# Moving the query's transposes and block sums into the second product, two scores forward, and one matrix load behind its scatters

## The chip, the cores and the metric

The kernel runs on one NeuronCore of a Trainium2 chip. It uses five engines with instruction streams of their own: TensorE (PE, matmuls and transposes), VectorE (DVE), ScalarE (ACT), GpSimd (POOL, here mostly gathers and scatters) and SyncE (SP, which issues most transfers). The metric is the device time of one execution in microseconds (us). Before the change it is 3199.84 us, the median of three runs (3196.97 to 3201.5).

## The reference, cut to what matters

Four graph layers, each with a residual and a layer norm, on x of 128 batches x 128 nodes x 256 features, all float32. Cut to the first layer, which the change touches, and its frame:

```python
# --- layer 0: attention over 512 edges, 4 heads of 64
Xq = (H @ W_lin.T).reshape(bt, n, h, dh)
Xv = (H @ W_val.T).reshape(bt, n, h, dh)
e = einsum('behd,hd->beh', leaky_relu(Xq[:, src] + Xq[:, dst], 0.2), a) + log(A0[src, dst] + EPS)
attn = exp(e - segment_max(e, src)) / segment_sum(...)       # softmax over the edges of one source
Y = segment_sum(attn * Xv[:, dst], src) ;  out = Y @ W_out.T
x = layernorm(x + out)
# --- layer 1: three products, each mixed over the nodes with adj * adj, relu after two of them
h = relu(mix(x @ W1)); h = relu(mix(h @ W2)); x = layernorm(x + mix(h @ W3))   # 256-512-1024-256
# --- layer 2: x @ W[k] for k = 0..2, mixed with diagonal, upper and lower triangle, + bias, layernorm
# --- layer 3: normalized adjacency, two linear maps with batch norm over all 128*128 rows, layernorm
```

## The kernel before

The 128 batches are worked in 32 quads of 4. A main loop has one round for each quad, and in round k five quads are in work at once: k-1 (`a`: layer 2, layer 3), k (`c`: second and third product of layer 1), k+1 (`b`: aggregation, first product), k+2 (`e`: scores and softmax) and k+3 (`g`: query and value product). The order of each engine's instructions is the order of the Python calls; waits between engines follow from the data.

Large products are done as seven block products in place of eight (Strassen-Winograd), with sums of blocks (S1 to S4, T1 to T4) made beforehand:

```python
class Seven:                      # y, z, x are PSUM banks; part() keeps a copy, out() writes a result
    def p1(self): self.y = ps("y"); self.mm(self.y, "A11", "B11", True); self.k1 = self.part(self.y, 0)
    def p5(self): self.z = ps("z"); self.mm(self.z, "S1", "T1", True)
    def p2(self): x = ps("x");      self.mm(x, "A12", "B21", True);      self.out(0, 0, x, self.k1)
    def p6(self): self.mm(self.y, "S2", "T2", False); self.k2 = self.part(self.y, 1)
    ...                           # p7, p4, p3 likewise

def values_in(k, xg, copy=None):  # transposes of x: 8 on PE into two banks, two copies on DVE
    for j in range(0, QB, 2):
        pt = ps("pt")...
        ... nc.tensor.transpose(pt[:, t, c, :], xg[:, j + t, c * P:(c + 1) * P], ident)      # L245
        xt = temp("xt")...;  copy(xt, pt);  s.xts.append(xt)                                 # L247

def node_blocks(tiles, room):     # the four sums of the left side, on DVE (L181 to L184)
    ...
    sums_a(a, a)

def queries(k, room):             # query and value product of quad k
    ...
    a = node_blocks(s.xts, room)
    def part(bank, i):
        nc.scalar.copy(room[2 + i], bank);  return room[2 + i]                               # L306
    return Seven(node_product(a, queries.blocks), part, out)

def temp(name):                   # six buffers
    return wk.tile([P, 512], F32, tag="t", name=name, bufs=6)
```

A score of one chunk of 128 edges is three DVE instructions on 128x1024 (the last chunk has one more):

```python
def score(k, c, weight=None):
    nc.vector.scalar_tensor_tensor(z, z, SLOPE, z, op0=ALU.mult, op1=ALU.max)                # L365
    nc.vector.tensor_mul(z3, z3, a_bc...)                                                    # L367
    nc.vector.reduce_sum(s.es[:, c, :], z..., axis=AX.X)                                     # L368
    ... elif c == NE - 1: nc.vector.tensor_add(s.es, s.es, log_col...)                       # L372
```

The attention weights are scattered into a matrix in DRAM and read back:

```python
def scatter(k, load=True):
    for c in range(NE): nc.gpsimd.indirect_dma_start(out=ad, ..., in_=s.at[:, c, :])         # L415
    if load: load_weights(k)      # nc.sync.dma_start(s.ad, ad...), 1 MB                     # L424
```

The second product of layer 1 has 14 block products, two halves g = 0, 1 of seven. Each is 4 matmuls of 512 columns (8 records of 256 columns in the profile). `between[i]` holds other work that is called at place i:

```python
def second(k, between):
    def keep(to, g, name):  to[g] = temp(name)...;  nc.scalar.copy(to[g], y[g])              # L578
    def total(g, row, col, bank, kept_): nc.vector.tensor_add(block(g, row, col), bank[g], kept_[g])  # L584
    def relu(g, row, col, src_=None): nc.scalar.activation(h, ..., AF.Relu)                  # L588

    product(y, 0, "A11", B11); keep(p1, 0, "p1");                                   after(0)
    product(y, 1, "A11", B11); keep(p1, 1, "p1");                                   after(1)
    product(x, 0, "A12", B21); total(0, 0, 0, x, p1);                               after(2)
    product(z, 0, "S1", T1);                                                        after(3)
    product(y, 0, "S2", T2);   keep(u2, 0, "u2");                                   after(4)
    product(y, 1, "S2", T2);   keep(u2, 1, "u2"); relu(0, 0, 0);                    after(5)
    product(x, 1, "A12", B21); total(1, 0, 0, x, p1);                               after(6)
    product(y, 0, "S3", T3);   keep(u3, 0, "u3"); total(0, 1, 1, z, u3); relu(1, 0, 0); after(7)
    product(z, 1, "S1", T1);                                                        after(8)
    product(y, 1, "S3", T3);   keep(u3, 1, "u3"); total(1, 1, 1, z, u3); relu(0, 1, 1); after(9)
    product(y, 0, "A22", T4);  relu(0, 1, 0, y[0]);                                 after(10)
    product(z, 0, "S4", B22);  total(0, 0, 1, z, u2); relu(1, 1, 1);                after(11)
    product(y, 1, "A22", T4);  relu(1, 1, 0, y[1]); relu(0, 0, 1);                  after(12)
    product(z, 1, "S4", B22);  total(1, 0, 1, z, u2); relu(1, 0, 1);                after(13)
```

One round, cut:

```python
def iteration(k):
    steps = softmax_parts(e)      # generator: [PE transpose L382, 4 ACT copies] [DVE scan L386] [scan L388]
                                  #   [DVE sub L391] [ACT exp L393] [DVE scan] [DVE scan]
    for i in (0, 1, 2, 3, 5, 7):          between[i] += [next(parts)]          # rest of layer 2 of quad a
    between[11] += [next(steps)];         between[12] += [next(steps)] * 2
    for c_, i in enumerate((0, 3, 6)):    between[i] += [score(e, c_ + 1)]
    for j, i in enumerate((5, 8, 9, 10)): between[i] += [by_row(b, j)]         # ACT copies, L434
    between[13] += [values_in(g, quads[g].xg)]
    second(c, between)
    quads[g + 1].xg = load_x(g + 1, "xg", 1, xpool)
    room = room_of("m2", 7)       # the buffer of the second product's right side, free from here on
    next(steps)
    q = queries(g, room[:5])
    stage_f(a)                    # PE L790 into two banks, two ACT copies (L793)
    h = hidden(a, room[5:] + room[2:4])   # layer 3, another seven block products (L819), its sums L188 to L191
    q.p1(); next(steps); run(q.p5, q.p2, q.p6); run(h.p1, h.p5); next(steps); q.p7(); ...
    spill(g)                      # query rows to DRAM (L268), then gather(g): 6 of the 8 gathers (L333)
    ...                           # aggregation, third product, first product, head of layer 2
```

Rounds 1 to 28 have a quad g, rounds 1 to 29 a quad e. The start, before the loop, does the first three quads by hand. Cut to what the change touches:

```python
    attention(0)
    scatter(0, False)
    ...                           # values(2, 0..3); the last one spills quad 2 (L268)
    values_in(3, quads[3].xg, nc.scalar.copy)
    quads[4].xg = load_x(4, "xg", 1, xpool)          # L205
    load_weights(0)                                  # L424
    score(1, 1, ...); ...
    for j in range(QB): by_row(0, j, ...)            # L434, on ACT and DVE by turns
    aggregate(0)                                     # PE L448
```

Of the kernel before, what the change touches and what calls it, by code (L numbers as in the profile page):

```python
# [26 lines left out]
def gnn_stack(ctx: ExitStack, tc: tile.TileContext, x, adj, w_qv_t, a, w_out_t, src, dst,  # L27
# [14 lines left out]
    nc = tc.nc  # L42
    B, N, D = x.shape
# [21 lines left out]
    def ps(name):  # L65
        return psum.tile([P, 512], F32, tag="ps", name=name)
# [62 lines left out]
    with ExitStack() as phase:  # L129
# [103 lines left out]
        def temp(name):  # L233
            return wk.tile([P, 512], F32, tag="t", name=name, bufs=6)
# [43 lines left out]
        def node_blocks(tiles, room):  # L278

            a = {f"A{j + 1}{c + 1}": tiles[j][:, :, c, :] for j in range(2) for c in range(2)}  # L280
            for i in range(4):
                a[f"S{i + 1}"] = room[i // 2][:, (i % 2) * 256:(i % 2 + 1) * 256].rearrange("p (b n) -> p b n", b=2)
            sums_a(a, a)
            return a

        def node_product(a, b):
            def mm(bank, i, j, new):
                for t in range(2):
                    nc.tensor.matmul(bank[:, t * 256:(t + 1) * 256], a[i][:, t, :], b[j],
                                     start=new and t == 0, stop=t == 1, skip_group_check=True)  # L290
            return mm
# [5 lines left out]

        def queries(k, room):

            s = quads[k]  # L300
            s.qt = wk.tile([P, QB, D], F32, tag="xb", name=f"qt{k}", bufs=1)
            s.xv = ws.tile([P, QB, D], F32, tag="xv", name=f"xv{k}", bufs=3)
            a = node_blocks(s.xts, room)

            def part(bank, i):
                nc.scalar.copy(room[2 + i], bank)  # L306
                return room[2 + i]

            def out(row, col, bank, kept_):
                to = (s.qt, s.xv)[col][:, 2 * row:2 * row + 2, :].rearrange("p b d -> p (b d)")  # L310
                if kept_ is None:
                    nc.scalar.copy(to, bank)
                else:
                    nc.vector.tensor_add(to, bank, kept_)

            return Seven(node_product(a, queries.blocks), part, out)

# [238 lines left out]
        def second(k, between):  # L556
# [3 lines left out]
            y, z, x = [None] * 2, [None] * 2, [None] * 2  # L560
            p1, u2, u3 = [None] * 2, [None] * 2, [None] * 2

# [12 lines left out]

            def keep(to, g, name):
                to[g] = temp(name).rearrange("p (i b n) -> p i b n", i=2, b=2)
                nc.scalar.copy(to[g], y[g])  # L578
# [15 lines left out]

            product(y, 0, "A11", B11)
            keep(p1, 0, "p1")
            after(0)
            product(y, 1, "A11", B11)
            keep(p1, 1, "p1")
            after(1)  # L600
# [5 lines left out]
            product(y, 0, "S2", T2)  # L606
            keep(u2, 0, "u2")
            after(4)
            product(y, 1, "S2", T2)
            keep(u2, 1, "u2")  # L610
            relu(0, 0, 0)
# [4 lines left out]
            product(y, 0, "S3", T3)  # L616
            keep(u3, 0, "u3")
            total(0, 1, 1, z, u3)
# [4 lines left out]
            product(y, 1, "S3", T3)  # L623
            keep(u3, 1, "u3")
            total(1, 1, 1, z, u3)
# [52 lines left out]
        def layer2(k, b):  # L678
# [52 lines left out]
            def mix(p):  # L731
                po = ps("po2").rearrange("p (t d) -> p t d", d=D)
                for i in range(2):
                    nc.tensor.matmul(po, split_t[:, i, :], g[p][:, :, (i + 1) * D:(i + 2) * D],
                                     start=(i == 0), stop=(i == 1))
                return po
# [22 lines left out]
            if b is not None:  # L759
                mixed(b, 2, pm[2])  # L760
                mixed(b, 3, pm[3])
            run(u.p1, u.p2, u.p5, u.p6, v.p1, v.p2, u.p7, v.p5, v.p6, u.p4, u.p3, v.p7)
            yield
            scaled(0)
# [114 lines left out]
        def run(*parts):  # L879
            for p in parts:  # L880
                p()

        def iteration(k):
# [11 lines left out]
            if has_c:  # L895
                between = {i: [] for i in range(14)}
                for i in (0, 1, 2, 3, 5, 7):
                    between[i].append(lambda: next(parts, None))
                between[11].append(lambda: next(steps, None))
                between[12] += [lambda: next(steps, None)] * 2  # L900
                if has_e:
                    for c_, i in enumerate((0, 3, 6)):
                        between[i].append(lambda c_=c_: score(e, c_ + 1))
                if has_b:
                    for j, i in enumerate((5, 8, 9, 10)):
                        between[i].append(lambda j=j: by_row(b, j))
                if has_g:
                    between[13].append(lambda: values_in(g, quads[g].xg))
                second(c, between)
# [8 lines left out]
            if has_g:  # L918
                q = queries(g, room[:5])
            stage_f(a)  # L920
# [123 lines left out]
        def start():  # L1044
# [136 lines left out]
            attention(0)  # L1181
            scatter(0, False)

# [28 lines left out]
            quads[4].xg = load_x(4, "xg", 1, xpool)  # L1212
            load_weights(0)
            score(1, 1, ends[:, 3, :])
# [343 lines left out]
```

## Time and profile before

| what | value |
|---|---|
| time, median of 3 | 3199.84 us |
| span of the profiled execution | 3199.8 us |
| TensorE clock granted, mean | 0.992 |
| one round, score transpose to score transpose | 87.37 us |
| ScalarE, GpSimd busy | 44%, 20% |
| memory traffic over the span | 105 GB/s |

The page of the profile shows the busy time of each engine and, for each kind of instruction, what ended the idle time before it. A line such as

```profile
L571 PE MATMUL ph<-m,w_s 128*128 128x256 f32 x1536 | 360.5, 381 | 11.9 <-DVE h L584 11.9
L578 ACT COPY u<-ph 128x512 f32<-128x512 f32 x128 | 74.9, 585 | 371.8 <-PE ph L571 371.8
L434 ACT COPY adc<-ad 128x512 f32<-128x512 f32 x126 | 134.9, 1071 | 8.3 <-DMA ad<-attd 8.3
```

reads: source line, engine and operation; output and inputs by name; shapes and number; then total busy time and the mean of one in ns; then the engine's idle time just before such instructions, and what ended it. The first is a part of the second product: 1536 matmuls of 381 ns as recorded (their records overlap, so the time from one start to the next is shorter), with 11.9 us of idle TensorE that ended when VectorE finished line 584. The second shows the other kind of waiting: ScalarE is idle 371.8 us before its copies, because it is ahead of TensorE. In the timeline, rows of the same kind are merged: start, duration, engine, line, names, shapes, number, and in brackets the idle time before and its end.

### The profile page before, as it was taken

How to read it: one execution, taken by the hardware profiler on the slowest of the kernel's cores; microseconds unless marked ns; L12 is line 12 of the kernel's file. 1: busy time of each engine (PE TensorE's matmuls, PEld its weight loads, DVE VectorE, ACT ScalarE, POOL GpSimd, SP SyncE). 2: the span in 40 equal slices, each digit the busy share in tenths (PEclk: the TensorE clock that was granted, in tenths of full speed). 3: DMA queues.
4: the chain of work that ended last, by engine and by line, in shares of the span. 5: the costliest groups of instructions: out<-in, count | busy, mean ns of one | idle time of the engine just before them, and what ended most of it. 6: DMA issues, size and time to landing. Idle time of an engine off the chain costs nothing. (4 is left out here: it accounts for less than half of the span.)

```text
span 3199.8 us, 39789 instructions
## 1 busy us (share of the span) xinstructions
PE 3105.5 (97%) x14760; PEld 2407.4 (75%) x14760; DVE 2301.8 (72%) x4598; ACT 1392.7 (44%) x2549; POOL 646.2 (20%) x533
## 2 busy tenths in 40 slices
PE   7999999999999999999999999999999999989998
PEld 3778887888888888888888888887888887864444
DVE  6777777777777777777777777777767776448888
ACT  3344433444444444433444444444433344326668
POOL 3211222222111111222222121111222220001135
PEclk8999999999999999999999999999999999999999
DMA  7423333333333323333333323323333331005557
GB/s 232 102 72 81 100 100 99 106 106 106 99 80 106 96 83 86 100 99 100 106 106 106 100 80 106 95 80 85 105 100 100 106 106 41 20 27 185 177 190 277
DMA packets 117472, 340.04 MB, mean 106 GB/s; under 512 B 14880, under 2 KB 51616, under 8 KB 108960
## 3 DMA queue, kind: packets, MB, share of 16 engines
q0 software_dynamic: 44400, 147.35, 18.9%
q1 hardware_dynamic: 71120, 189.23, 16.6%
q8 instruction: 117, 1.92, 0.2%
q10 hardware_dynamic: 1760, 0.92, 0.1%
q14 instruction: 75, 0.61, 0.1%
HBM read 252.00 MB, written 85.46 MB: 105 GB/s over the span
## 5 line engine op out<-in xcount | busy, mean ns | idle before, releaser
L571 PE MATMUL ph<-m,w 128*128 128x256 f32 x2048 | 473.1, 379 | 0.0
L652 PE MATMUL p<-w,h 128*128 128x256 f32 x2048 | 464.1, 380 | 0.0
L571 PEld LDWEIGHTS ph<-m,w 128*128 128x128 f32 x2048 | 386.8, 190 | 80.0 <-issue 14.8
L652 PEld LDWEIGHTS p<-w,h 128*128 128x128 f32 x2048 | 389.8, 190 | 67.1 <-issue 8.1
L333 POOL DMA_INDIRECT zs<-qd,src_idx x120 | 115.6, 963 | 1409.0 <-DMA qd<-qt 1275.5
L571 PE MATMUL ph<-m,w_s 128*128 128x256 f32 x1536 | 360.5, 381 | 11.9 <-DVE h L584 11.9
L571 PEld LDWEIGHTS ph<-m,w_s 128*128 128x128 f32 x1536 | 289.4, 190 | 75.0 <-DVE h L584 23.5
L333 POOL DMA_INDIRECT zs<-qd,dst_idx x120 | 189.4, 1578 | 346.9 <-DMA zs<-qd,src_idx 338.3
L578 ACT COPY u<-ph 128x512 f32<-128x512 f32 x128 | 74.9, 585 | 371.8 <-PE ph L571 371.8
L415 POOL DMA_INDIRECT attd<-at,att_idx x128 | 140.8, 1100 | 349.4 <-DMA attd<-at,att_idx 253.6
L113 ACT ACTIVATE ln_sd<-ln_mv,eps 128x2 f32<-128x2 f32 x192 | 56.0, 292 | 279.4 <-DVE ln_mv L108 279.4
L588 ACT ACTIVATE h<-h 128x512 f32<-128x512 f32 x192 | 121.0, 630 | 118.1 <-DVE h L584 118.1
L367 DVE TENSOR_TENSOR zs<-zs,a_bc 128x1024 f32<-128x1024 f32 x125 | 153.2, 1225 | 4.3
L368 DVE TENSOR_REDUCE scores<-zs 128x16 f32<-128x1024 f32 x125 | 152.5, 1220 | 4.3
L715 ACT COPY x2k<-y 128x384 f32<-128x384 f32 x192 | 91.8, 478 | 141.1 <-PE y L708 113.5
L365 DVE SCALAR_TENSOR_TENSOR zs<-zs 128x1024 f32<-128x1024 f32 x125 | 151.5, 1212 | 0.2 <-DMA zs<-qd,dst_idx 0.2
L106 DVE BATCH_NORM_STATS2 ln_st<-xr 128x6 f32<-128x256 f32 x384 | 144.6, 419 | 6.6
L121 DVE TENSOR_SCALAR xr<-xr,ln_mv,ln_rs 128x256 f32<-128x256 f32 x384 | 143.5, 416 | 7.0
L434 ACT COPY adc<-ad 128x512 f32<-128x512 f32 x126 | 134.9, 1071 | 8.3 <-DMA ad<-attd 8.3
L119 DVE RECIPROCAL ln_rs<-ln_sd 128x2 f32<-128x2 f32 x192 | 31.3, 163 | 148.0 <-ACT ln_sd L113 148.0
L676 POOL TENSOR_TENSOR xb<-xr,bias 128x512 f32<-128x512 f32 x64 | 99.1, 1548 | 168.3 <-DVE xr L121 150.8
L529 PE MATMUL pm<-wt_t,h 128*128 128x128 f32 x1024 | 128.8, 279 | 0.0
(336 smaller groups left out, 6144.7 us busy)
## 6 DMA issues: line engine op xcount, KB each, us to landing
ad<-attd SPq DMA_DIRECT2D x32, 1024.0 KB, 4.8
zd<-z SPq DMA_DIRECT2D x31, 1024.0 KB, 7.4
zl<-zd SPq DMA_DIRECT2D x62, 512.0 KB, 3.6
xr<-in_x_dram SPq DMA_DIRECT2D x32, 512.0 KB, 7.1
x3d<-xr SPq DMA_DIRECT2D x32, 512.0 KB, 2.6
x3l<-x3d SPq DMA_DIRECT2D x32, 512.0 KB, 5.1
out_dram<-x3l POOLq DMA_DIRECT2D x31, 512.0 KB, 5.7
qd<-qt SPq DMA_DIRECT2D x30, 512.0 KB, 2.6
```

Source lines behind the costliest of these rows:

```text
L106: nc.vector.bn_stats(st[:, i, :], r[:, i, :])
L121: nc.vector.tensor_scalar(r[:, i, :], r[:, i, :], mv[:, i, 0:1], rs[:, i:i + 1], op0=ALU.subtract, op1=ALU.mult)
L333: nc.gpsimd.indirect_dma_start(out=s.z[c], out_offset=None, in_=s.qd, in_offset=bass.IndirectOffsetOnAxis(ap=idx[:, c:c + 1], axis=0), com ...
L365: nc.vector.scalar_tensor_tensor(z, z, SLOPE, z, op0=ALU.mult, op1=ALU.max)
L367: nc.vector.tensor_mul(z3, z3, a_bc.unsqueeze(1).to_broadcast([P, QB, D]))
L368: nc.vector.reduce_sum(s.es[:, c, :], z.rearrange("p (r d) -> p r d", d=DH), axis=AX.X)
L415: nc.gpsimd.indirect_dma_start(out=ad, out_offset=bass.IndirectOffsetOnAxis(ap=att_idx[:, c:c + 1], axis=0), in_=s.at[:, c, :], in_offset= ...
L434: (copy or nc.scalar.copy)(s.adc[:, j * H:(j + 1) * H, :], s.ad.rearrange("p (s r) -> p r s", r=R)[:, j * H:(j + 1) * H, :])
L529: nc.tensor.matmul(pm[:, c // 2, c % 2, :], quads[k].h1[i, c], wt_t, start=True, stop=True)
L571: nc.tensor.matmul(bank[g][:, i].rearrange("p b n -> p (b n)"), wa[:, c, f:f + P], s.m2[:, blk_b, c].rearrange("p b n -> p (b n)"), start= ...
L588: nc.scalar.activation(h, h if src_ is None else src_, AF.Relu)
L652: nc.tensor.matmul(p3[:, t * D:(t + 1) * D], s.h2[f // 2][:, f % 2, j + t, :], w3_sb[:, f, :], start=(f == 0), stop=(f == K2 - 1))
```

## The change

It has four parts. The transposes of x for the next query product, and the four block sums made of them, move from behind the second product to its place 11, two block products before its end. The sums get two temporary tiles in place of the room that comes free only after the second product. The second and third of the three scores in the second product move from places 3 and 6 to places 2 and 4. In the start, the load of the first attention matrix goes directly behind its scatters in the queue, ahead of a spill and a load of x. To make the buffers come out, the kept tiles of the second product are taken all at once at its beginning, and the two PSUM banks for the mixing of layer 2 before it. No computation is added or removed. The aim is that TensorE finds its inputs ready.

```diff
-        def queries(k, room):
+        def queries(k, kept_at):
             s = quads[k]
+            blocks = quads[k].x_blocks
             ...
-            a = node_blocks(s.xts, room)
             def part(bank, i):
-                nc.scalar.copy(room[2 + i], bank)
-                return room[2 + i]
+                nc.scalar.copy(kept_at[i], bank)
+                return kept_at[i]
             ...
-            return Seven(node_product(a, queries.blocks), part, out)
+            return Seven(node_product(blocks, queries.blocks), part, out)
+
+        def query_sums(k):
+            quads[k].x_blocks = node_blocks(quads[k].xts, [temp("xs") for _ in range(2)])
 ...  # second()
-            p1, u2, u3 = [None] * 2, [None] * 2, [None] * 2
+            p1, u3, u2 = ([temp(name).rearrange("p (i b n) -> p i b n", i=2, b=2) for _ in range(2)]
+                          for name in ("p1", "u3", "u2"))
-            def keep(to, g, name):
-                to[g] = temp(name).rearrange("p (i b n) -> p i b n", i=2, b=2)
+            def keep(to, g):
                 nc.scalar.copy(to[g], y[g])
 ...  # layer2()
-                po = ps("po2").rearrange("p (t d) -> p t d", d=D)
+                po = pos[p]
 ...
             run(u.p1, u.p2, u.p5, u.p6, v.p1, v.p2, u.p7, v.p5, v.p6, u.p4, u.p3, v.p7)
+            pos = [ps("po2").rearrange("p (t d) -> p t d", d=D) for _ in range(2)]
             yield
 ...  # iteration()
                 between[11].append(lambda: next(steps, None))
+                if has_g:
+                    between[11] += [lambda: values_in(g, quads[g].xg), lambda: query_sums(g)]
 ...
-                    for c_, i in enumerate((0, 3, 6)):
+                    for c_, i in enumerate((0, 2, 4)):
                         between[i].append(lambda c_=c_: score(e, c_ + 1))
 ...
-                if has_g:
-                    between[13].append(lambda: values_in(g, quads[g].xg))
                 second(c, between)
 ...
-                q = queries(g, room[:5])
+                q = queries(g, room[:3])
 ...  # start()
-            scatter(0, False)
+            scatter(0)
 ...
             quads[4].xg = load_x(4, "xg", 1, xpool)
-            load_weights(0)
             score(1, 1, ends[:, 3, :])
```

More of the change, by code (lines that the diff above doesn't have):

```diff
@@ L595, in second @@
             product(y, 0, "A11", B11)
-            keep(p1, 0, "p1")
+            keep(p1, 0)
             after(0)
             product(y, 1, "A11", B11)
-            keep(p1, 1, "p1")
+            keep(p1, 1)
             after(1)
@@ L606, in second @@
             product(y, 0, "S2", T2)
-            keep(u2, 0, "u2")
+            keep(u2, 0)
             after(4)
             product(y, 1, "S2", T2)
-            keep(u2, 1, "u2")
+            keep(u2, 1)
             relu(0, 0, 0)
@@ L616, in second @@
             product(y, 0, "S3", T3)
-            keep(u3, 0, "u3")
+            keep(u3, 0)
             total(0, 1, 1, z, u3)
@@ L623, in second @@
             product(y, 1, "S3", T3)
-            keep(u3, 1, "u3")
+            keep(u3, 1)
             total(1, 1, 1, z, u3)
```

## The prediction

> **What bounds the kernel now.** I read the page first (engine shares, slices), then the list of waits for TensorE, then the timeline of one round of the main loop, engine by engine, and last the start. The chain of waits on the page is of no help here: it covers only the last 1.7 us.
>
> ```profile
> PE 3105.5 (97%) x14760; PEld 2407.4 (75%) x14760; DVE 2301.8 (72%) x4598; ACT 1392.7 (44%) x2549; POOL 646.2 (20%) x533
> PE   7999999999999999999999999999999999989998
> ```
>
> TensorE (PE) is the bound in nearly all of the 40 slices: 3199.8 - 3105.5 = 94 us of idle time are all that any rearrangement can win, unless it takes matmuls away, and this change takes none away. So the first question is where TensorE stands still:
>
> ```profile
> PE z L289 <- DVE m L181: 13.7, 28, 0.5
> PE ph L571 <- DVE h L584: 11.9, 29, 0.4
> PE py L448 <- ACT adc L434: 8.1, 1, 8.1
> ```
>
> Columns: total us, times, longest. The three longest waits of TensorE are just the three things the change works on: L181 is the first of the block sums of x for the query product (28 rounds have one), L584 is `total` in the second product (29 rounds have scores in them), and L434 at L448 is the first attention matrix in the start.
>
> Idle time understates them, because the end of a matmul record is modelled. I therefore measure from start to start, in one round from the middle:
>
> ```profile
> 1252.67 1.89 PE L571 MATMUL ph<-m,w_s 128*128 128x256 f32 x8
> 1254.39 3.62 PE L571 MATMUL ph<-m,w 128*128 128x256 f32 x16
> 1258.42 1.99 PE L571 MATMUL ph<-m,w_s 128*128 128x256 f32 x8 [0.41 <-DVE h L584]
> ...
> 1263.82 1.04 PE L245 MATMUL pt<-ident,xg 128*128 128x128 f32 x8
> 1264.69 1.95 PE L790 MATMUL pa<-ahat_t,xr 128*128 128x128 f32 x16
> 1266.67 1.13 PE L289 MATMUL y<-wqv,xt 128*128 128x256 f32 x4
> 1268.30 1.10 PE L289 MATMUL z<-wqv,m 128*128 128x256 f32 x4 [0.49 <-DVE m L181]
> 1269.23 1.03 PE L289 MATMUL x<-wqv,xt 128*128 128x256 f32 x4
> 1270.10 1.03 PE L289 MATMUL y<-wqv_s,m 128*128 128x256 f32 x4
> ```
>
> First and second column: start and duration. A block product of 8 matmuls takes 1.72 us (1252.67 to 1254.39), so 16 should take 3.44; from 1254.39 to 1258.42 are 4.03. Lost: 0.58 us. Eight transposes take 0.87 (1263.82 to 1264.69), so the 16 matmuls of L790, of the same shape, should take 1.74; 1264.69 to 1266.67 is 1.98. Lost: 0.24, in which the query product waits for the copy of the transposes. Four matmuls take 0.87 (1269.23 to 1270.10); 1266.67 to 1268.30 is 1.63. Lost: 0.76, the wait for the sums.
>
> **What the Trainium skill says.** "Perfetto Trace Analysis", section "Identifying the Most-Contended Engine", calls the share of busy matmul time a poor measure and asks for the share of weight loads. Here that is 75%, and the matmuls follow each other without a hole all the same: the 0.216 us of a 128x256 float32 matmul sets the pace and the 0.19 us weight load hides under it. The same page, "Tensor Engine Instruction (MATMUL, LD_WEIGHTS)", says that a matmul's end in the profile is estimated; the trace agrees, as the wait listed with 0.49 us costs 0.76. It also says there that ACT and DVE work strictly in order; the DVE rows below show it. "ScalarE: Activation LUTs", section "What ACT_TABLE_LOAD costs", gives 1283 ns a load and a drain of about 1380 more: the trace has 1283, but the next activation starts 1.29 us after the load, so no drain is seen here. "DMA: Bandwidth & Descriptors", section "Issuing engines are not separate DMA queues", says that transfers from all engines share the same 16 DMA engines and interleave; the start below fits that.
>
> **The change part by part: scores sooner.** Why does `total` come late? VectorE (DVE) in the same round:
>
> ```profile
> 1250.74 0.17 DVE L119 RECIPROCAL ln_rs<-ln_sd 128x2 f32<-128x2 f32 x1 [2.31 <-ACT ln_sd L113]
> ...
> 1253.78 1.22 DVE L365 SCALAR_TENSOR_TENSOR zs<-zs 128x1024 f32<-128x1024 f32 x1
> 1255.03 1.23 DVE L367 TENSOR_TENSOR zs<-zs,a_bc 128x1024 f32<-128x1024 f32 x1
> 1256.29 1.22 DVE L368 TENSOR_REDUCE scores<-zs 128x16 f32<-128x1024 f32 x1
> 1257.54 0.22 DVE L372 TENSOR_TENSOR scores<-scores,log_col 128x64 f32<-128x64 f32 x1
> 1257.68 0.68 DVE L584 TENSOR_TENSOR h<-ph,u 128x512 f32<-128x512 f32 x1
> ```
>
> The last score (3.9 us, 1253.78 to 1257.68) stands ahead of the `total` that frees bank z, and product S4 must wait for it; before that DVE had 2.31 us with nothing to do. From place 6 to place 4 the score moves ahead of L119, into that hole. By hand: score 1248.4 to 1252.3; normalizations and L740 to L108, which now take 1250.74 to 1253.20, from 1252.3 to 1254.8; `total` of x to 1255.4; `total` of z to 1256.0. S4 comes up at 1254.39 + 3.44 = 1257.8, so 1.8 us are to spare and the 0.58 go whole: x29 = 16.8 us. Moving the middle score from 3 to 2 changes nothing: between the two places DVE has no other instruction. The price is on ScalarE (ACT): a relu behind the delayed `total` of x waits until 1255.4, so the copy of u3 ends at 1257.8 instead of 1256.9; its reader on TensorE (A22 of the second half) comes after S4, the transpose of the scores and the transposes of x, at 1260.7. Nothing lost.
>
> **Transposes and sums into the second product.** The 8 transposes keep their 0.87 us on TensorE and only change places with two block products: no gain by themselves. What is gained is that the copy and the sums are done before they are asked for: 0.24 + 0.76 = 1.00 us x 28 = 28 us. The cost is one of order on DVE: two copies (0.6 each) and four sums (0.36 from start to start, 1267.75 to 1269.20) now stand ahead of the two scans and of the last `total`. By hand, from S4 at 1257.8: it ends near 1259.7; `total` to 1260.35; copies to 1261.6; sums to 1263.0; scans (2.4) to 1265.4; the last `total` to 1266.0, as late as now (1265.37 + 0.65), while TensorE is 1.6 us ahead. ACT then does relu, two copies of the aggregate and the copy of the query's first part: 0.55 + 1.05 + 0.6, to about 1268.3. TensorE asks for that copy after y, z and x of the query product: it begins y at 1264.1 + 1.74 = 1265.85 and needs the bank back at 1265.85 + 3 x 0.87 = 1268.45. That is a slack of 0.1 us, which I cannot tell from a small wait. The next reuse of the bank is as tight: table load and exponential (1.28 + 0.6) end at 1270.2, the copy behind them at 1270.8, and it is wanted at 1271.05. I take 0.1 us a round as the residual: 28 x 0.1 = 3 us lost.
>
> **The other places.** The two banks for the mixing of layer 2 are taken before the second product, and its six kept tiles at its beginning. That changes names of buffers; on TensorE no new wait arises whose producer comes late in the timeline. The sums get two more temporary tiles out of six, whose earlier readers are through by then.
>
> **Matrix load behind the scatters (once).**
>
> ```profile
> 62.60 0.99 POOL L415 DMA_INDIRECT attd<-at,att_idx  x1 [4.21 <-DMA attd<-at,att_idx]
> 67.61 1.89 POOL L415 DMA_INDIRECT attd<-at,att_idx  x1 [4.02 <-DMA attd<-at,att_idx]
> 70.91 0.96 POOL L415 DMA_INDIRECT attd<-at,att_idx  x1 [1.42 <-DMA attd<-at,att_idx]
> ```
>
> Each scatter waits for the one before. They are 5.0 and 3.3 us apart here and 2.4 apart at 104.9 to 109.7. In the SyncE queue two transfers of 512 KB (the spill of quad 2 at 62.31, x of quad 4 at 62.78) run beside the second one, ahead of the matrix load, which goes out at 73.01. Issued behind the scatters, the matrix load holds both back: scatters at 62.6, 65.0 and 67.4, load at 69.5, 3.5 us sooner, and at the head of the queue. It now takes 6.1 us with a spill and three gathers in flight; the page's median is 4.8. I put it at 5.6, so TensorE's wait of 8.1 us shrinks by 3.5 + 0.5 = 4 us. The price: the gathers of quad 2 now start near 77 instead of 72.6, and land well before their first score after 110.
>
> Sum: 16.8 + 28 - 3 + 4 = 46 us; 3199.84 - 46 = 3154 us.
>
> **Rivals.** (a) *VectorE takes over as the bound at the end of the second product.* For it: from S4 on DVE is full for 11 us in my schedule and the slack at the query's bank is 0.1 us. If each estimate there is 0.3 us too low, 0.5 us a round come back, 14 us: about 3165. Against it: DVE is only 72% busy, and the hole of 1.84 us ahead of the scans (they wait for ACT's pair copies) takes in most of the moved work. (b) *The waits only move within the round*, because something with a fixed period (gathers, scatters, matrix load) paces it: near 3195. Against it: GpSimd waits some 50 us of each 87.37 us round for the spill, and the last gather, issued at 1227.6 and taking about 7 us, has landed over 10 us before the earlier score at 1248.4. (c) *Only the listed idle time is won*: 13.7 + 11.9 + 4 = 30 us, 3170. Against it: the distances from start to start. (d) *The start gives nothing*, as the matrix load shares its time with the two transfers right behind it: 4 us less, 3158.
>
> **Range and chances.** All waits removed and a good start: 45 + 5, 3150; with the spread of the runs before (3196.97 to 3201.5) 3146. Rival (a) with (d) gives 3169, rival (c) 3170; so 3146 to 3172 for 8 in 10. A gain of 2% is 64 us, more than the 45 + 8 us that these waits hold together: 0.03. Slower by 2% would need over 2 us of new wait in every round beyond what is won: 0.02. Within 2%: 0.95.
>
> **What would show it.** Right: the waits on L181's and L584's successors gone from TensorE's list; score transposes 85.9 us apart instead of 87.37; the first attention matrix 4 us sooner. Wrong: a new line "PE y <- ACT m" of 28 times at the query product (rival a), or "PE <- DVE h" again with 29.

## The result and the profile after

The changed kernel takes 3156.95 us (median of 4 runs, 3156.04 to 3160.04), the kernel before 3199.02 (4 runs, 3196.97 to 3201.5). The ratio is 0.987, 95% interval 0.9853 to 0.9887: 42 us, 1.3%. Line numbers of the changed kernel are 3 or 4 higher: L571 became L575, `total` L584 became L587, L790 became L794, L819 became L823, L448 became L451.

The page of the changed kernel, busy time:

```profile
PE 3086.7 (98%) x14760; PEld 2409.3 (76%) x14760; DVE 2317.5 (73%) x4598; ACT 1378.4 (44%) x2549; POOL 647.5 (21%) x533
```

The instruction counts of TensorE and VectorE are unchanged. But VectorE is busy 15.7 us longer than before (2301.8) with the same 4598 instructions. That is a first hint of something that the change did not intend; the held instructions found below make up some 10 us of it.

TensorE's waits after (total us, times, longest):

```profile
PE pt L1451 <- ACT agg L1293: 10.9, 6, 3.3
...
PE py L451 <- ACT adc L437: 3.8, 1, 3.8
...
PE y L711 <- ACT x2k L718: 2.6, 5, 0.6
```

The two waits of every round, for the sums of L181 and for `total`, are no longer in the list, and the wait in the start fell from 8.1 to 3.8 us. The first line, in the output stage, was 7.6 us before; it grew. The third is small and comes only 5 times: it will lead to the cause of a few long rounds.

TensorE in one round after, the stretch that answers to the one shown of before:

```profile
1233.72 3.62 PE L575 MATMUL ph<-m,w 128*128 128x256 f32 x16
1237.17 1.89 PE L575 MATMUL ph<-m,w_s 128*128 128x256 f32 x8
1238.90 0.27 PE L385 MATMUL pe<-ident,scores 128*128 128x128 f32 x1
1239.01 1.04 PE L245 MATMUL pt<-ident,xg 128*128 128x128 f32 x8
...
1243.34 1.95 PE L794 MATMUL pa<-ahat_t,xr 128*128 128x128 f32 x16
1245.12 1.03 PE L289 MATMUL y<-wqv,xt 128*128 128x256 f32 x4
1245.99 1.03 PE L289 MATMUL z<-wqv,xs 128*128 128x256 f32 x4
...
1247.72 1.11 PE L289 MATMUL y<-wqv_s,xs 128*128 128x256 f32 x4
1248.66 1.03 PE L823 MATMUL y<-ag,l3w 128*128 128x256 f32 x4
```

From start to start: 16 matmuls of L575 take 3.45 us (4.03 before), the 16 of L794 1.78 (1.98), from the query's y to its z 0.87 (1.63). Each stands at or near the pace of its matmuls. In the last two lines something new shows: 0.94 us between starts where four matmuls take 0.86, a loss of 0.08.

VectorE and ScalarE (ACT) in the same round:

```profile
1231.44 0.23 DVE L375 TENSOR_TENSOR scores<-scores,log_col 128x64 f32<-128x64 f32 x1
...
1234.60 0.68 DVE L587 TENSOR_TENSOR h<-ph,u 128x512 f32<-128x512 f32 x1
...
1239.71 1.28 DVE L247 COPY xt<-pt 128x512 f32<-128x512 f32 x2
1241.02 0.42 DVE L181 TENSOR_TENSOR xs<-xt 128x256 f32<-128x256 f32 x1
...
1244.88 0.65 DVE L587 TENSOR_TENSOR h<-ph,u 128x512 f32<-128x512 f32 x1
```

```profile
1245.57 0.63 ACT L591 ACTIVATE h<-h 128x512 f32<-128x512 f32 x1 [2.63 <-DVE h L587]
...
1247.05 0.60 ACT L306 COPY m<-y 128x512 f32<-128x512 f32 x1
```

The last score is done at 1231.6 and `total` of z at 1235.28, well before S4 is due at 1237.17. The sums begin at 1241.02, 4.1 us ahead of the query product. ScalarE's copy of the query's first part ends at 1247.65, just when TensorE asks for that bank again: its row at 1247.72 is 1.11 us long in place of 1.03, and that is the 0.08.

Measured from score transpose to score transpose, the regular round went from 87.37 to 85.74 us. There are 29 such distances; the first one, into the loop, is short (62.9 and 62.8), so 28 regular rounds follow. The profiled executions split as follows:

| us | before | after | difference |
|---|---|---|---|
| start, to the first score transpose | 148.97 | 144.59 | -4.4 |
| loop, first to last score transpose | 2510.02 | 2466.88 | -43.1 |
| tail, from the last one to the end | 540.81 | 543.88 | +3.1 |
| span | 3199.8 | 3155.35 | -44.5 |

28 rounds by 1.63 us are 45.6 us; the loop gained 2.5 us less. Four of its rounds after are longer than the rest (86.45 to 86.72), before there was one (88.26). Three rounds in a row, the first and the third of them long, in a table of windows (us; busy time and instructions of the engines; clock; share of the DMA engines; GB/s):

```profile
core 0: us, PE busy (x) PEld busy (x) DVE busy (x) ACT busy (x) POOL busy (x), PEclk, DMA share, GB/s
293.15:379.70 86.55, 86.02 (x435) 70.51 (x434) 65.59 (x125) 35.75 (x68) 16.86 (x14) 1.00 0.34 98
379.70:465.44 85.74, 85.74 (x435) 70.63 (x433) 63.38 (x125) 35.82 (x68) 16.68 (x14) 1.00 0.36 99
465.44:552.16 86.72, 86.04 (x435) 70.54 (x434) 65.69 (x125) 35.84 (x68) 17.45 (x14) 1.00 0.35 98
```

The engines issue the same number of instructions (the weight loads differ by one), but in the long rounds VectorE is busy 2.2 to 2.3 us longer with its 125. So one or more of them took longer. In the timeline of VectorE in the first of these rounds it is found at once:

```profile
346.53 0.28 DVE L181 TENSOR_TENSOR x2s<-x2t 128x128 f32<-128x128 f32 x1
346.84 2.56 DVE L182 TENSOR_TENSOR x2s<-x2s,x2t 128x128 f32<-128x128 f32 x1
349.32 0.28 DVE L183 TENSOR_TENSOR x2s<-x2t 128x128 f32<-128x128 f32 x1
```

One addition of 128x128 in the block sums of layer 2, usually 0.29 us, took 2.56. GpSimd (POOL) at that time:

```profile
346.35 1.58 POOL L336 DMA_INDIRECT zs<-qd,dst_idx  x1 [6.46 <-DMA zs<-qd,src_idx]
347.38 1.86 POOL L679 TENSOR_TENSOR xb<-xr,bias 128x512 f32<-128x512 f32 x1
```

The last gather of the round, and directly behind it a bias addition which ends at 349.24. VectorE goes on at 349.32. TensorE then waits 0.54 us at 352.21 for a copy (the third line of its waits). The output stage has the same picture: a VectorE instruction on 128x4, `nm<-mv,rs` (0.16 us), takes 1.39, 1.08, 1.87 and 0.89 us in four of its 32 cases after and 1.40 and 1.07 in two cases before, each time beside an addition on GpSimd, and TensorE waits 1.6 us for each. This was the theory for the experiments below: *VectorE is held by GpSimd's addition where it has two inputs in SBUF.* "SBUF — State Buffer" in the Trainium skill, section "Who interferes with whom", says just this: "A DVE instruction with two SBUF inputs contends with a GpSimd instruction that reads SBUF". The trace adds the size, and that VectorE is held although its row begins 0.54 us ahead of the addition's (rows of GpSimd are rough).

### The profile page after: what moved, and what is told of

The parts are those of the page before. It is cut to its first block, busy times and chain, and to the rows that moved or that the text cites. A ratio compares the mean times of both kernels' runs of the same rounds, so it can differ in the third digit from the quotient of the medians.

```text
span 3155.3 us, 39760 instructions
## 1 busy us (share of the span) xinstructions
PE 3086.7 (98%) x14760; PEld 2409.3 (76%) x14760; DVE 2317.5 (73%) x4598; ACT 1378.4 (44%) x2549; POOL 647.5 (21%) x533
## 3 DMA queue, kind: packets, MB, share of 16 engines
q8 instruction: 117, 1.92, 0.3%
## 5 line engine op out<-in xcount | busy, mean ns | idle before, releaser
L575 PE MATMUL ph<-m,w 128*128 128x256 f32 x2048 | 473.1, 379 | 0.0
L575 PEld LDWEIGHTS ph<-m,w 128*128 128x128 f32 x2048 | 386.8, 190 | 77.9 <-issue 14.8
L575 PE MATMUL ph<-m,w_s 128*128 128x256 f32 x1536 | 357.5, 379 | 0.0
L575 PEld LDWEIGHTS ph<-m,w_s 128*128 128x128 f32 x1536 | 291.8, 190 | 52.9 <-issue 14.8
L121 DVE TENSOR_SCALAR xr<-xr,ln_mv,ln_rs 128x256 f32<-128x256 f32 x384 | 142.4, 413 | 7.0
L587 DVE TENSOR_TENSOR h<-ph,u 128x512 f32<-128x512 f32 x128 | 87.0, 680 | 71.0 <-PE ph L575 50.9
```

What stands on the lines that cost most here:

```text
L121: nc.vector.tensor_scalar(r[:, i, :], r[:, i, :], mv[:, i, 0:1], rs[:, i:i + 1], op0=ALU.subtract, op1=ALU.mult)
L575: nc.tensor.matmul(bank[g][:, i].rearrange("p b n -> p (b n)"), wa[:, c, f:f + P], s.m2[:, blk_b, c].rearrange("p b n -> p (b n)"), start= ...
```

## The experiments

"Loop" is the distance from the first to the last score transpose in the profiled execution, "round" its regular distance. The runs of before beside them had medians of 3199.97 to 3202.98 us.

**The scores alone.** The kernel before, with one line changed:

```diff
-                    for c_, i in enumerate((0, 3, 6)):
+                    for c_, i in enumerate((0, 2, 4)):
```

> The kernel before with the scores alone at places 0, 2 and 4. Theory (each wait is worth its start-to-start distance, and the parts add up): the 0.58 us ahead of product S4 and the 0.10 us ahead of the score transpose go in 29 rounds, 20 us, so about 3179 us, and score transposes 86.7 us apart in place of 87.37. Rival (only the listed idle time is won): 12 us, 3187. Rival (the waits move within the round, the query product then waits longer for its sums): under 5 us.

Measured: 3178.64 us (3173.26 to 3181.32), ratio 0.9925 (0.9907 to 0.9944). Loop 2486.48, rounds 86.50: 0.87 us a round. That is more than the 0.58 of the wait for `total`. TensorE in a round of this kernel:

```profile
1158.49 3.62 PE L571 MATMUL ph<-m,w 128*128 128x256 f32 x16
1161.95 1.89 PE L571 MATMUL ph<-m,w_s 128*128 128x256 f32 x8
1163.67 0.27 PE L382 MATMUL pe<-ident,scores 128*128 128x128 f32 x1
...
1168.11 1.95 PE L790 MATMUL pa<-ahat_t,xr 128*128 128x128 f32 x16
1169.90 1.13 PE L289 MATMUL y<-wqv,xt 128*128 128x256 f32 x4
1171.53 1.10 PE L289 MATMUL z<-wqv,m 128*128 128x256 f32 x4 [0.49 <-DVE m L181]
```

The wait for `total` is gone (3.46 in place of 4.03), 0.10 goes between S4 and the transpose of the scores (1.72 in place of 1.83), and 0.19 at the query product: 1.79 from L790 to y in place of 1.98, although the transposes and their copies are where they were. The reason lies in ScalarE. Its rows and the score transpose, first in the kernel before, then here:

```profile
1258.40 0.63 ACT L588 ACTIVATE h<-h 128x512 f32<-128x512 f32 x1 [1.50 <-DVE h L584]
...
1260.25 0.27 PE L382 MATMUL pe<-ident,scores 128*128 128x128 f32 x1
...
1261.90 1.05 ACT L384 COPY pair<-pe 16x128 f32<-16x128 f32 x4
```

```profile
1165.13 1.04 ACT L384 COPY pair<-pe 16x128 f32<-16x128 f32 x4
```

Before, a relu waited 1.50 us for the late `total` and pushed the copies of the score pairs back. They began 1.65 us after the score transpose (1260.25 to 1261.90), here 1.46 (1163.67 to 1165.13). The scans wait for them, the last `total` for the scans, the copies of the transposes for that. The wait of 0.49 for the sums stays as it was (28 times, 13.7 us).

**The last score alone.**

```diff
-                    for c_, i in enumerate((0, 3, 6)):
+                    for c_, i in enumerate((0, 3, 4)):
```

> As the run before it, but the middle score stays at place 3 and only the last one goes from 6 to 4. Theory: the middle score changes nothing, as VectorE has no other instruction between its two places: the same time as with both, within 2 us, about 3179. Rival (sooner is better for each score): some 5 us slower than with both.

Measured: 3176.36 us (3172.5 to 3177.81), ratio 0.9925 (0.9909 to 0.9942). Loop 2485.83, rounds 86.50. The whole gain of the scores is that of the last one; moving the middle one does nothing.

**The transposes and sums alone.** The changed kernel with the scores and the start put back:

```diff
-                    for c_, i in enumerate((0, 2, 4)):
+                    for c_, i in enumerate((0, 3, 6)):
 ...
-            scatter(0)
+            scatter(0, False)
 ...
+            load_weights(0)
```

> The transposes and block sums at place 11 with their buffers, scores at the old places 0, 3 and 6, the start as before. Theory (additive): 0.24 + 0.76 + 0.07 less 0.08 at the copy of the query's first part, 28 rounds, 28 us: about 3171, and the wait on line 584's total ahead of S4 still there 29 times with 0.4. Rival (the earlier score makes the room on VectorE for the moved work; without it the sums come late again): under 20 us gained, over 3179.

Measured: 3173.67 us (3172.18 to 3178.66), ratio 0.9921 (0.9903 to 0.9938). Loop 2484.07, rounds 86.42: 0.95 us a round. TensorE in a round:

```profile
1154.00 3.62 PE L575 MATMUL ph<-m,w 128*128 128x256 f32 x16
1158.02 1.99 PE L575 MATMUL ph<-m,w_s 128*128 128x256 f32 x8 [0.41 <-DVE h L587]
...
1164.29 1.95 PE L794 MATMUL pa<-ahat_t,xr 128*128 128x128 f32 x16
1166.07 1.03 PE L289 MATMUL y<-wqv,xt 128*128 128x256 f32 x4
1166.94 1.03 PE L289 MATMUL z<-wqv,xs 128*128 128x256 f32 x4
```

The wait for `total` is there as before (29 times, 11.9 us), the waits at the query product are gone: 1.78 and 0.87. The two parts together (0.87 + 0.95) would be 1.82 a round; both together gave 1.63. The difference is the 0.19 at the query product, which either part takes away and which is counted twice.

**The start alone.**

```diff
-            scatter(0, False)
+            scatter(0)
 ...
-            load_weights(0)
```

> The kernel before with the matrix load directly behind the scatters alone. Theory: the first attention matrix comes 4.3 us sooner and nothing after gives it back: 3195 us, first score transpose at 144.6 in place of 149.0. Rival (the later spill and the later gathers of quad 2 give it back in the first rounds): 3199, first score transpose sooner but the second one not.

Measured: 3201.04 us (median of 12, 3194.9 to 3205.76), ratio 0.9997 (0.9988 to 1.0006). The total neither shows a gain nor excludes one of 3 us. Over all profiles of this study the part itself can be read: TensorE waits for the first attention matrix 8.1, 7.8, 6.8 and 5.4 us in the four with the old start (mean 7.05), and 3.5 to 5.8 (mean 4.8) in the ten with the new one. So by this wait the part is worth about 2.2 us, from four traces against ten, whose ranges overlap. The whole stretch up to the first score transpose of the loop spreads more than that: 143.9 to 149.0 us with the old start, 141.1 to 148.1 with the new one. The four scatters explain the spread: from the first of them to the load it takes 13.3 to 15.6 us in the old order and 11.3 or 13.3 in the new one. From the load to TensorE's start it takes 7.0 to 7.3 us in both: being at the head of the queue made the load itself no faster.

**The buffers.** The changed kernel, with the kept tiles taken where they are filled and the two banks for the mixing taken in `mix`, as in the kernel before:

```diff
-                po = pos[p]
+                po = ps("po2").rearrange("p (t d) -> p t d", d=D)
 ...
+                to[g] = temp("kept").rearrange("p (i b n) -> p i b n", i=2, b=2)
```

> The changed kernel with the banks of layer 2's mixing and the kept tiles of the second product taken where they were taken before. Theory: the places of the buffers cost and bring nothing, the rounds are 85.74 us again. Rival (a bank of the transposes or a tile of the sums then has a late reader): a new wait at the transposes or at place 11, rounds of over 86 us.

Measured: 3157.72 us (3154.52 to 3160.08), ratio 0.9859 (0.9842 to 0.9877), rounds 85.74, loop 2466.26. The order in which buffers are taken makes no difference that these runs show.

**The gather sooner.** A first test of the theory of the held instruction: the first of the two bias additions on GpSimd goes from ahead of the last gather to behind it. The gather then comes sooner, and its second part, now with both additions behind it, falls on the block sums in many rounds. If the theory holds, these rounds become long.

```diff
-            third_norm(c, 0)
+            third_norm(c, 0, not has_g)          # without the addition
 ...
                 gather_last(g)
+                third_bias(c, 0, nc.gpsimd)      # the addition
```

> The changed kernel with one GpSimd addition (the first half of the bias of layer 2) put behind the first part of the last gather in place of ahead of it, so that the gather comes 1.4 us sooner and its second part falls on the block sums of layer 2 on VectorE. Theory (VectorE held): many rounds, some 15 to 25 of 28, get a block sum of about 2.5 us in place of 0.29 and become 0.7 to 0.9 us longer, so 3168 to 3180 us. Rival (the few long block sums are chance, or come from memory traffic): as many long rounds as before, 3 or 4, and 3157 us.

Measured: 3205.7 us (median of 12, 3201.59 to 3214.88), ratio 1.0012 (1.0003 to 1.002): the whole gain of the change is lost, more than expected. Loop 2520.54 in the profiled execution, which was the longest of the twelve (3214.88); rounds of 86.6 to 89.8. VectorE and GpSimd in one of 87.8 us:

```profile
1049.25 0.28 DVE L183 TENSOR_TENSOR adc<-x2t 128x128 f32<-128x128 f32 x1
1049.45 3.80 DVE L184 TENSOR_TENSOR adc<-x2t,adc 128x128 f32<-128x128 f32 x1
```

```profile
1048.98 1.59 POOL L336 DMA_INDIRECT zs<-qd,dst_idx  x1 [4.84 <-DMA zs<-qd,src_idx]
1050.00 3.10 POOL L684 TENSOR_TENSOR xb<-xr,bias 128x512 f32<-128x512 f32 x2
```

The two additions now follow one another, 3.1 us, and fall on the expected sums (`x2s`), on the sums one step earlier (`adc`, as here), or on the normalization L121. In each of the 28 rounds, where 15 to 25 were expected, at least one of them is held, for 2.1 to 3.9 us. So the holds can be brought about at will, and one costs more where two additions follow one another. L121 does not fit the theory as it is worded: it has one tensor as input, and two columns with one value for each partition (`ln_mv`, `ln_rs`), all in SBUF. In this kernel it was held in all 8 cases in which it ran beside an addition. Which of its operands matters was not tested.

**The bias addition on VectorE.** The addition behind the gather goes to VectorE itself, between the block products of layer 2:

```diff
-                third_norm(c, 2)
+                third_norm(c, 2, False)
 ...
-            run(u.p1, u.p2, u.p5, u.p6, v.p1, v.p2, u.p7, v.p5, v.p6, u.p4, u.p3, v.p7)
+            run(u.p1, u.p2, u.p5, u.p6, v.p1, v.p2, u.p7, v.p5, v.p6,
+                lambda: third_bias(k, 2, nc.vector), u.p4, u.p3, v.p7)
```

> The changed kernel with the second half of that bias addition on VectorE, into a hole of 1.5 us it has in the products of layer 2, so that no GpSimd addition stands behind the last gather. Theory (VectorE held): no long block sums, all rounds 85.7 us, 3 us less than the changed kernel, about 3154. Rival (chance or traffic): a few long rounds as before, no gain.

The changed kernel unchanged was the control in the same group of runs:

> The changed kernel once more, beside the three variants of it. All theories: 0.987 of the kernel before. Theory on the lost rest (VectorE is held whenever one of its instructions with two SBUF inputs meets GpSimd between a gather and the addition behind it): the rounds that are longer than 85.74 us, here again a few, are just those in which the last gather begins between 0.3 us before and 0.3 us after the block sums of layer 2; which rounds they are changes from run to run.

Measured: 3153.03 us (3149.56 to 3155.77), ratio 0.9844 (0.9827 to 0.9862); the control 3155.39 (3147.89 to 3156.29), ratio 0.9848 (0.9827 to 0.9868). The times alone do not tell the two apart. The profiles do: the control has two long rounds (86.67 and 86.66), each with a block sum held (2.53 and 2.67 us); without GpSimd's addition all are 85.74 but for one of 85.92. Four times the gather began within 0.15 us ahead of the sums, close to where they were held in the control (0.22 us ahead and 0.03 behind), and no sum took longer. So it is the addition that holds VectorE, and not the gather.

**The query's first product early.** For the 0.08 us in each round: the query's y goes ahead of the aggregate product, so that ScalarE copies it ahead of the two aggregate copies.

```diff
                 q = queries(g, room[:3])
+                q.p1()
             stage_f(a)
 ...
-            if has_g:
-                q.p1()
```

> The changed kernel with one more move: the first block product of the query (y, with ScalarE's copy of its first part k1) goes ahead of the two aggregate products of layer 3 in the order of calls. Theory (the 0.08 us that TensorE now loses between the query's p6 and the hidden layer's p1 is ScalarE's copy of k1 standing behind two aggregate copies of 0.5 us each): with the copy first the 0.08 us goes, rounds become 85.66 us in place of 85.74, 28 x 0.08 = 2.2 us in all. Rival: the aggregate copies now end 0.6 us later, and their readers, the hidden layer's first product and its sums on VectorE, turn this into a new wait in every round (rounds of 85.8 or more, a line of some 28 times on TensorE for the hidden layer's sums).

**Both small gains together,** with the changed kernel as the control in the same group:

> The changed kernel with the query's first block product ahead of the aggregate products and the bias addition behind the last gather on VectorE in place of GpSimd. Theory: both small gains add, rounds of 85.66 us throughout with none above 86.2, loop 3 to 5 us shorter than that of the changed kernel, about 3151 us. Rival: the additions on VectorE (0.6 us more work a round at the end of the first product) or the later aggregate copies cost what is won: 3155 us or more.

> The changed kernel unchanged, as the control on the same chip: 3155 us, rounds of 85.74 us with one to four of 86.4 to 86.8 where VectorE's block sums of layer 2 are held beside GpSimd's last gather.

Measured: first product early 3155.5 us (3148.69 to 3159.97), ratio 0.9848 (0.9835 to 0.9861); both 3152.72 (3147.5 to 3154.75), ratio 0.9845 (0.9831 to 0.9858); control 3156.74 (3155.17 to 3159.89), ratio 0.9858 (0.9843 to 0.9873). The rounds of the first are 85.66 with three of 86.6 to 86.9, those of both 85.66 with a single one of 85.84, those of the control 85.74 with four of 86.4 to 86.8. Each effect is there in the rounds; the intervals of the times overlap. TensorE with the query first:

```profile
1247.34 1.03 PE L289 MATMUL y<-wqv_s,xs 128*128 128x256 f32 x4
1248.20 1.03 PE L823 MATMUL y<-ag,l3w 128*128 128x256 f32 x4
```

0.86 us, the pace of its matmuls, in place of 0.94. And a round of the kernel with both, in which the gather begins 0.06 us ahead of the sums, VectorE and GpSimd:

```profile
941.90 0.28 DVE L181 TENSOR_TENSOR x2s<-x2t 128x128 f32<-128x128 f32 x1
942.21 0.29 DVE L182 TENSOR_TENSOR x2s<-x2s,x2t 128x128 f32<-128x128 f32 x1
```

```profile
941.84 1.59 POOL L336 DMA_INDIRECT zs<-qd,dst_idx  x1 [6.57 <-DMA zs<-qd,src_idx]
```

No hold. In this kernel the output stage had five (1.31 to 1.91 us), so its tail is 544.05 us, and what the loop wins (2460.64) is partly hidden by them.

**One input from PSUM in the output stage.** The test from VectorE's side: the addition on GpSimd stays, but `nm` reads one of its two inputs from PSUM. It is the kernel with both small gains, and one reciprocal more:

```diff
                 nc.vector.reciprocal(rs, coefs[q])
-                nc.vector.scalar_tensor_tensor(nm, mvs[q][:, :, 0], -1.0, rs, op0=ALU.mult, op1=ALU.mult)
+                rp = ps("shift_ps")[:, :QB]
+                nc.vector.reciprocal(rp, coefs[q])
+                nc.vector.scalar_tensor_tensor(nm, mvs[q][:, :, 0], -1.0, rp, op0=ALU.mult, op1=ALU.mult)
```

> The kernel with both small gains (query's first product early, bias addition on VectorE), and in the output stage the reciprocal is made a second time into PSUM, so that the product nm (128x4) reads one input from SBUF and one from PSUM in place of two from SBUF. Theory (VectorE is held beside GpSimd's addition only where it has two inputs in SBUF): none of the nm instructions is longer than 0.2 us, where 5 of 32 took 1.3 to 1.9 us in the kernel with both; the line of TensorE waiting for agg falls from 12.1 us to about 4 or less, the tail from the last score transpose on is 5 x 1.6 = 8 us shorter, less 32 x 0.15 us on VectorE that lie in its idle time: about 537 us in place of 544.1; the time near 3146 us. Rival (GpSimd's issue of the output, or its addition, holds any instruction of VectorE): nm is still held in 2 to 7 places and the tail stays at 540 to 545 us.

Measured: 3146.69 us (5 runs, 3146.07 to 3147.67), ratio 0.9834 (0.982 to 0.9847). The tile `nm` in this kernel (ns, shortest, median, longest of 32):

```profile
L1485 DVE SCALAR_TENSOR_TENSOR nm<-mv,shift_ps x32: 157/157/158, 3044.0 to 3139.1; 128x4 f32<-128x4 f32 x32
```

None is held. But only two of the 32 ran beside an addition at all: they began within 0.1 us of its start. In the other 13 profiles 48 of these instructions ran beside one, and all 48 were held. The extra reciprocal also moves `nm` in time by about 0.1 us, so part of what this kernel gains may be that it meets fewer additions. The better evidence for PSUM is an instruction that nobody changed. The addition `x3l<-x3l,pt` of the output stage (128x512, `pt` in PSUM) began while an operation of GpSimd ran 332 times in the 14 profiles, and never took more than its usual 0.69 us.

TensorE's wait in the output stage, in the kernel with both small gains and in this one:

```profile
PE pt L1455 <- ACT agg L1297: 12.1, 7, 3.3
```

```profile
PE pt L1455 <- ACT agg L1297: 5.4, 4, 3.3
```

6.7 us less, and the tail falls from 544.05 to 538.36. The median is the lowest of all versions. But the kernel with both small gains was measured in another group, beside a kernel before that was 3 us slower (3202.98 against 3199.97), and the intervals of the two ratios overlap. So the gain of this step is shown by the profiles and not by the times.

## Why the prediction was right, and where its steps were off

The predicted 3154 us lie 3 us below the measured median of 3156.95, which is well inside the predicted range. That the total came so near is partly luck: the regular rounds gained 3.8 us more than predicted (45.6 in place of 16.8 + 28 - 3 = 41.8), and long rounds and holds that nobody foresaw took 5.5. Each step, in the order of the prediction:

- **Start-to-start distances instead of listed idle time (rival c).** Right. The three listed waits hold 30 us in all, the change gave 42. The distances promised 0.58, 0.24 and 0.76 us a round; after the change 0.01, 0.04 and 0 of them are left. For the same reason the 94 us of idle time, which the prediction took for all that can be won, were no ceiling. TensorE's idle time fell by 25.7 us only (94.3 to 68.6), and its busy time, with the same 14760 matmuls, by 18.8: part of each wait stood in the records as busy.
- **Scores sooner, 16.8 us.** Right in mechanism; the term was too small. Alone it gave 23.5 us in the loop (0.87 a round). The prediction followed VectorE only as far as S4 and did not follow the late `total` through ScalarE's relu to the pair copies, the scans and the query product, where it costs another 0.19, and 0.10 ahead of the score transpose. That the middle score does nothing was right.
- **Transposes and sums, 28 us.** Right for the part alone (0.95 a round). But the sum treated it as independent of the scores: 0.19 of it is the same wait that the scores remove. The two errors nearly cancel: 1.58 predicted, 1.71 measured (1.63 and the 0.08 given back).
- **Residual of 0.1 us a round at the query's bank.** Right: 0.08, and calling the product early removed it. The schedule by hand placed the end of ScalarE's copy against TensorE's demand within 0.1 us, so rival (a), VectorE as the new bound with 0.5 us a round, did not come about.
- **The start, 4 us.** In the two profiles compared it was 4.4; TensorE's wait over all profiles says 2.2. The step that failed is the 0.5 us for a load at the head of the queue, and to some degree the 3.5 for the scatters: the old order varies by itself from 13.3 to 15.6 us, and the profile of before was at its long end. Rival (d) was half right.
- **New names of buffers, no new wait.** Right.
- **Not foreseen:** long rounds (four after, one before) and holds in the output stage (four after, two before), together about 5.5 us between the two profiles (2.4 and 3.1). Their mechanism is in the kernel before too. Block sums were held in one to three of the 28 regular rounds in the profiles of before and of one part alone, and in two to four in those of the changed kernel, so they are not shown to be a cost of the change; the phase decides on which instruction GpSimd's addition falls. Without them the gain between these two profiles would have been near 50 us in place of the predicted 46.

What stays open: why the scatters of the start take one of two lengths (11.3 or 13.3 us) in the new order, and which operands of L121 let GpSimd hold it. Neither was tried.

## What to carry to other kernels

Read a wait from start to start at the pace of its matmuls, and follow the late instruction through every engine that waits for it: two changes that remove the same wait do not add up. Where an engine has a hole of 2 us ahead of a late piece of work, moving the piece into it is safe if the next demand on each bank is followed by hand to 0.1 us. When rounds of the same instructions differ in length, compare the busy time of each engine between them; an instruction of VectorE with both inputs in SBUF beside an addition on GpSimd is one to look for, and the addition moved to another engine removed it here (none of 15 cases held), as an input from PSUM seems to.

## What the runs showed of the hardware that was not expected

A short instruction of VectorE with two inputs in SBUF is held until GpSimd's addition of 128x512 ends: 0.29 us become 2.4 to 2.7 behind a gather, up to 3.9 beside two additions, and 0.16 up to 1.92 for 128x4. Take all profiles with the addition directly behind the gather (the one of the sooner gather left aside). The gather began between 0.44 us ahead of the start of the sums and 0.34 us behind it in 25 rounds; in each of them a sum was held, and it ended 0.16 us behind the addition. In the three kernels without that addition the gather began so in 15 rounds, and no sum was held. VectorE counts the held time as busy: it does not appear among its waits, and only the duration tells it.

Two things in the same traces widen this. First, a hold can be there every time, and then the longest is no longer than the median: in the last product of layer 3 the subtraction L1351 (128x1024, both inputs in SBUF) takes 2.81 to 3.18 us in all 15 cases, beside GpSimd's subtraction L1353; L1355, of the same shape and without GpSimd beside it, takes 1.20 to 1.23. The kernel before has the same. Second, it goes both ways: where VectorE began first, GpSimd was held. L1201 and L1203 of the start (128x128) took 0.30 and 0.29 us in the kernel before; in the changed one they begin 0.01 and 0.09 us behind two instructions of a score, take 1.35 and 1.29 us, and end 0.15 us behind them.
